# Moving ScalarE's share of the split forms within a unit, and an output's scaling across the seam between images (fp32 attention block, one core)

## The chip, the cores and the metric

The kernel runs on one core of a Trainium2 chip. The time is the device time of one execution in microseconds, the median of several runs. Engines are named as in the profile: PE (TensorE matmul), PEld (TensorE weight load), DVE (VectorE), ACT (ScalarE), POOL (GpSimd) and SP (SyncE). Each engine executes its own instructions in the order in which the program issues them, which for this kernel is written out by hand.

## The reference

The input is four images of 64 x 64 positions with 256 channels, in fp32. A layer computes self-attention in each image, and adds it to its input:

```python
q = jnp.einsum('bwhc,cd->bwhd', x, Wq) + bq      # 128 channels
k = jnp.einsum('bwhc,cd->bwhd', x, Wk) + bk      # 128 channels
v = jnp.einsum('bwhc,cd->bwhd', x, Wv) + bv      # 256 channels
pq = q.reshape(B, -1, N)                         # N = 4096
pk = k.reshape(B, -1, N)
pv = v.reshape(B, -1, N)
energy = jnp.einsum('bcn,bcm->bnm', pq, pk)
attention = jax.nn.softmax(energy, axis=-1)
out = jnp.einsum('bcm,bnm->bcn', pv, attention)
return gamma * out.reshape(B, W, H, C) + x
```

So for each image there is a 4096 x 4096 matrix of energies with 128 terms each, a softmax over its rows, and a product with v of 256 rows.

## The kernel before, in words

**Split operands.** Products of fp32 numbers are put together from three products of numbers in the faster fp32r format. Each operand of a product is split into three forms: a rounded one, what is left over, and a combination of both. The first form is an ACT instruction (a scaling that writes fp32r), the other two are DVE instructions that read the first. For q and k this is `halved` (ACT L263, DVE L265), for v it is `halve_v` (ACT L288 writes vh, DVE L291 writes vl and vd), and for the exponentials it is `upper` (ACT L343 writes h) and `halves` (DVE L349 writes l, L352 writes d).

**An image's work.** First its projection, 16 steps: PE transposes a part of x (tile xt, copied by ACT L130 into xts), multiplies it with the weights of q and k (tile qk, brought out by DVE L146 as qks) and of v (ACT L167). k's three forms and the plain q go to DRAM by DMA. After the projection come 128 units u, in 16 groups g of 256 rows of energies each, 8 units t to a group. A unit takes 512 columns.

**A unit.** In unit u the program issues, in this order: the energies of unit u + 3 (`LOOK`), in two halves k = 0 and 1; after the first half the `join` and `upper` of unit u + 2; then the steps of outputs in progress (`proceed`); `halves` of unit u + 1; in some units q's or v's forms; and `attend`, which multiplies unit u's h, l and d with vh, vl and vd. On each engine this comes to the following in a unit:

- PE: 12 matmuls for energies (tiles sa and sb, L324), then 24 for the output (tiles a with h and l, tile bb with d, L374).
- ACT: exponentials x and y of the first half (L328), h of unit u + 2 (L343), exponentials of the second half.
- DVE: the join of unit u + 2, x times y (L338), then l and d of unit u + 1 (L349, L352).

The tiles sa and sb have two buffers each in PSUM, so that PE may write the second half of the next unit's energies only when ACT has read the second half of this one's.

**The extra work in some units.** When the energies that a unit issues are the sixth unit of their group (`ahead % NU == 5`, which is u % 8 == 2) and there is a next group, the next group's q gets its forms: `halve_q`, 15 times an image (the first group's q is done in the projection). In units u = 1 and u = 3 of each image the last two parts of v get theirs: `halve_v`. In the kernel before both calls stand behind the whole energies of the unit, `proceed` and `halves`.

**Outputs.** A finished group's output goes through `finish`, a generator that takes one step at each `proceed`; a unit calls it twice. Its steps: ACT brings the sums out of PSUM (tile o, L385), DVE adds bb (L400), ACT scales by the reciprocal sums (L403), PE transposes (tile ot, L411), DVE adds the input (L415), and a DMA writes it. The last output of an image is in the middle of these steps when the next image's projection begins. Between the two images (called the seam below) stand these lines:

```python
            if b + 1 < B:
                proceed()
                images[b + 1].transposed(1)
                project_qk(b + 1, 0)
                proceed()
```

In the second `proceed` ACT issues the scaling of the last output (L403). `project_qk` issues q's and k's product and the forms of its k (ACT L263, which waits for qks).

Of the kernel before, what the change touches and what calls it, by code (L numbers as in the profile page):

```python
# [20 lines left out]
def kernel(  # L21
# [40 lines left out]
    C2 = C // 2  # L62
    NM = N // P
    KC = C // P
    NI = NM // 2
# [14 lines left out]
    def load_x(pool, b, g):  # L80
        t = pool.tile([P, 2, XB], F32, tag="x", name=f"x_{b}_{g}")
        nc.sync.dma_start(t, xv[b, g])
        return t
# [93 lines left out]
    NG = N // NB  # L177
    NU = NM // 4
# [22 lines left out]
    with ExitStack() as fast:  # L201
# [24 lines left out]
        images, qd, kf, units, loads, now = [], {}, {}, {}, {}, {}  # L226
# [5 lines left out]
        def start(pieces):  # L232
            active.append(pieces)
            next(pieces)

        def proceed():
            for pieces in list(active):
                if next(pieces, StopIteration) is StopIteration:
                    active.remove(pieces)
# [20 lines left out]
        def halved(f, x):  # L260

            h = f[:, :, 0, :]
            nc.scalar.activation(h, x, AF.Identity, scale=UPPER / 64)  # L263
            for j, s, op in ((1, -64.0, ALU.add), (2, 64.0 * (1.0 + E), ALU.subtract)):
                nc.vector.scalar_tensor_tensor(  # L265
                    f[:, :, j, :], h.bitcast(F32), s, x, ALU.mult, op
                )

        def project_qk(b, i):
            images[b].qk(i)  # L270
            x = now["qk"]
            for s in range(2):
                nc.gpsimd.dma_start(qd[b, i // 2 + NG // 2 * s][:, i % 2, :], x[:, s, :C2])  # L273
            f = kpool.tile([P, 2, 3, P], F32R, tag="f", name=f"f_{b}_{i}", bufs=2)
            halved(f, x[:, :, C2:])
            nc.gpsimd.dma_start(kf[b, i // 2][:, i % 2], f.rearrange("p s j d -> p s (j d)"))

        def project_v(b, i):
            images[b].v(i)
            units[b, "v4", i] = now["v4"]  # L280
            if i < NI - 2:
                halve_v(b, i)

        def halve_v(b, i):
            v4 = units.pop((b, "v4", i))
            m = slice(2 * i, 2 * i + 2)
            h = vh[:, m, :C]
            nc.scalar.activation(h, v4, AF.Identity, scale=UPPER * E)  # L288

            for t, f in ((vl, 1.0 / E), (vd, 1.0 / E + 1.0)):  # L290
                nc.vector.scalar_tensor_tensor(  # L291
                    t[:, m, :C], h.bitcast(F32), -f, v4, ALU.mult, ALU.add
                )

        def load_q(b, g):
            t = work.tile([P, NJ, P], F32, tag="qr", name=f"qr_{b}_{g}", bufs=1)
            nc.sync.dma_start(t, qd[b, g])
            loads[b, "qr", g] = t

        def halve_q(b, g):  # L300
            t = work.tile([P, 3, NJ, P], F32R, tag="q", name=f"q_{b}_{g}")
            halved(t.rearrange("p f j d -> p j f d"), loads.pop((b, "qr", g)))
            loads[b, "q", g] = t

        def load_k(b, u):
            if u < STEPS:
                t = kpool.tile([P, 4, 3, P], F32R, tag="k", name=f"k_{b}_{u}")
                nc.gpsimd.dma_start(t.rearrange("p (i s) f d -> p i s (f d)", s=2), kf[b, u % NU])  # L308
                loads[b, "k", u] = t

        def energy(b, u, k):

            g, t = divmod(u, NU)
            if k == 0:
                x = ppool.tile([P, 4, NB], F32, tag="x", name=f"x_{b}_{u}", bufs=3)
                y = ppool.tile([P, 4, NB], F32, tag="y", name=f"y_{b}_{u}")
                units[b, u] = x, y
            x, y = units[b, u]
            q, kt = loads[b, "q", g], loads[b, "k", u]
            sa = ps_s.tile([P, 2, NJ, P], F32, tag="a", name=f"sa_{b}_{u}_{k}")  # L320
            sb = ps_s.tile([P, 2, NJ, P], F32, tag="b", name=f"sb_{b}_{u}_{k}")
            for i in range(2):
                for to, f, first, last in ((sa, 0, True, False), (sa, 1, False, True), (sb, 2, True, True)):
                    nc.tensor.matmul(  # L324
                        to[:, i], kt[:, 2 * k + i, f, :], q[:, f], start=first, stop=last
                    )
            for to, sp, scale in ((x, sa, (1.0 + E) / E), (y, sb, -1.0 / E)):
                nc.scalar.activation(  # L328
                    to[:, 2 * k : 2 * k + 2, :],
                    sp.rearrange("p i j d -> p i (j d)"),  # L330
                    AF.Exp,
                    scale=scale,
                )

        def join(b, u):

            x, y = units[b, u]
            nc.vector.tensor_tensor(x, x, y, ALU.mult)  # L338
            units[b, u] = x

        def upper(b, u):
            h = ppool.tile([P, 4, NB], F32R, tag="h", name=f"h_{b}_{u}", bufs=3)
            nc.scalar.activation(h, units[b, u], AF.Identity, scale=UPPER)  # L343
            units[b, u] = units[b, u], h
# [117 lines left out]
        def begin(b, i):  # L462

            if i == 5:
                load_q(b, 0)
            if i == 9:
                halve_q(b, 0)
            if i in (4, 6, 8):
                load_k(b, i // 2 - 2)
            if i >= 10:  # L470
                energy(b, (i - 10) // 2, i % 2)
            if i in (12, 14):
                join(b, i // 2 - 6)
            if i in (13, 15):
                upper(b, i // 2 - 6)
                load_k(b, i // 2 - 3)

        image(0)
        for b in range(B):
            pr = images[b]  # L480
            if b == 0:
                now["banks"] = energies
                pr.transposed(0)
                pr.transposed(1)
                project_qk(b, 0)
            for i in range(1, NI):
                if i == 3:
                    now["banks"] = outputs
                if i + 1 < NI:
                    pr.transposed(i + 1)  # L490
                while i == 1 and active:
                    proceed()
                begin(b, i)
                project_qk(b, i)
                if i == NI - 1:
                    halves(b, 0)
                project_v(b, i - 1)
                proceed()
            project_v(b, NI - 1)
            for u in range(STEPS):  # L500
                g, t = divmod(u, NU)
                ahead = u + LOOK
                if ahead // NU + 1 < NG and ahead % NU == 3:
                    load_q(b, ahead // NU + 1)
                if u == STEPS - NU and b + 1 < B:
                    image(b + 1)
                if u >= STEPS - 3 and b + 1 < B:
                    now["banks"] = energies
                    if u == STEPS - 3:
                        images[b + 1].load(0)  # L510
                    elif u == STEPS - 2:
                        images[b + 1].transposed(0)
                if t == NU - 3:
                    loads[b, "x", g] = load_x(xpool, b, g)
                for k in range(2):
                    if ahead < STEPS:
                        energy(b, ahead, k)
                    if k == 0 and u + 2 < STEPS:
                        join(b, u + 2)
                        upper(b, u + 2)  # L520
                load_k(b, ahead + 2)
                proceed()
                if u + 1 < STEPS:
                    halves(b, u + 1)
                if ahead // NU + 1 < NG and ahead % NU == 5:
                    halve_q(b, ahead // NU + 1)

                if u in (1, 3):
                    halve_v(b, NI - 2 + u // 2)
                attend(b, u)  # L530
                if (b, u) == (B - 1, STEPS - 1):
                    finish_last(b, g, loads.pop((b, "x", g)))
                elif t == NU - 1:
                    start(finish(b, g, now["o"], now["bb"], loads.pop((b, "x", g))))
                proceed()
            if b + 1 < B:
                proceed()
                images[b + 1].transposed(1)
                project_qk(b + 1, 0)
                proceed()  # L540

    NB = 512
    NG = N // NB
# [3 lines left out]
    with tc.If(nc.values_load(again[0:1, 0:1]) > 0), ExitStack() as general:  # L547
# [8 lines left out]
        for b in range(B):  # L556
# [16 lines left out]
            for g in range(NG):  # L573
                ps = []
                mx = work.tile([P, 2, NB], F32, tag="mx", name=f"gmx_{b}_{g}")
                for t in range(NP):
# [9 lines left out]
                    p = ppool.tile([P, 2, NB], F32, tag="p", name=f"gp_{b}_{g}_{t}")  # L586
# [89 lines left out]
```

## Time and profile before

| | before |
|---|---|
| time, median of 3 runs | 2463.58 us (2461.89 to 2464.12) |
| span of the profiled execution | 2461.6 us |
| PE busy | 2444.7 us, 99% |
| PEld busy | 2410.5 us, 98% |
| DVE busy | 2096.1 us, 85% |
| ACT busy | 1802.1 us, 73% |
| POOL busy | 424.5 us, 17% |
| ACT, forms of q (L263, q) | 64 of 435 ns |
| ACT, forms of k (L263, f) | 64 of 417 ns |
| ACT, forms of v (L288, vh) | 64 of 630 ns |
| ACT, scalings of outputs (L403) | 126 of 527 ns |

Busy time is the time in which an engine had at least one instruction under way. An instruction's row gives the mean length of one. Instructions of one engine overlap a little, so that the step from one start to the next can be shorter than the length. Idle time in front of an instruction is put down to the engine and tile that released it last.

### The profile page before, as it was taken

The numbers are of one execution on the slowest core, as the hardware profiler recorded it, in microseconds if no ns is written. First come the engines' busy times: TensorE is split into PE (matmuls) and PEld (weight loads), VectorE is DVE, ScalarE is ACT, GpSimd is POOL, SyncE is SP. The second block draws the span as 40 slices with busy tenths as digits, with TensorE's granted clock in tenths as the row PEclk, the third lists the DMA queues.
The fourth block names the chain that finished last, engine by engine and source line by source line (L and its number), as shares of the span: only waits on it lengthen the run. The fifth ranks groups of instructions, "written<-read, shape, count | busy, mean of one in ns | idle before, by whom it ended". The sixth has DMA issues, their size and how long they took to land.

```text
span 2461.6 us, 50024 instructions
## 1 busy us (share of the span) xinstructions
PE 2444.7 (99%) x19982; PEld 2410.5 (98%) x19982; DVE 2096.1 (85%) x2314; ACT 1802.1 (73%) x3201; POOL 424.5 (17%) x781
## 2 busy tenths in 40 slices
PE   9999999999999999999999999999999999999998
PEld 8999999999899999999989999999998999999998
DVE  5888888888698888888869888888886988888887
ACT  5777777777677777777667777777766777777775
POOL 4211111111411111111141111111114111111110
PEclk9999999999999999999999999999999999999999
DMA  7666666665776666666477666666647766666663
GB/s 230 214 208 205 211 203 198 206 212 156 224 221 200 205 210 203 210 196 212 143 239 220 201 201 211 202 210 200 206 142 239 222 208 197 209 202 210 205 201 112
DMA packets 137408, 498.92 MB, mean 203 GB/s; under 512 B 15536, under 2 KB 57264, under 8 KB 137168
## 3 DMA queue, kind: packets, MB, share of 16 engines
q0 software_dynamic: 92320, 453.17, 59.1%
q1 hardware_dynamic: 44304, 42.22, 5.6%
q8 instruction: 160, 2.62, 0.4%
q14 instruction: 80, 0.66, 0.1%
q10 hardware_dynamic: 544, 0.26, 0.0%
HBM read 445.25 MB, written 50.33 MB: 201 GB/s over the span
## 4 chain that ended last, share of the span: by engine, by line


## 5 line engine op out<-in xcount | busy, mean ns | idle before, releaser
L328 ACT ACTIVATE x<-sa 128x512 f32<-128x512 f32 x1024 | 611.1, 597 | 498.1 <-PE sa L324 495.0
L338 DVE TENSOR_TENSOR x<-x,y 128x1024 f32<-128x1024 f32 x512 | 626.2, 1223 | 188.1 <-ACT y L328 188.1
L324 PE MATMUL sa<-q,k 128*128 128x256 f32 x4096 | 736.3, 279 | 1.1 <-ACT x L328 1.1
L352 DVE SCALAR_TENSOR_TENSOR d<-h,x 128x1024 fp32r<-128x1024 f32 x512 | 624.4, 1219 | 0.0
L349 DVE TENSOR_TENSOR l<-x,h 128x1024 fp32r<-128x1024 f32 x512 | 624.0, 1219 | 0.0
L324 PEld LDWEIGHTS sa<-q,k 128*128 128x128 f32 x4096 | 619.6, 188 | 2.2 <-ACT x L328 1.8
L328 ACT ACTIVATE y<-sb 128x512 f32<-128x512 f32 x1024 | 614.9, 600 | 0.0
L374 PE MATMUL a<-vh,h 128*128 128x258 f32 x4096 | 574.3, 283 | 0.0
L374 PE MATMUL a<-vl,l 128*128 128x258 f32 x4096 | 572.9, 282 | 0.0
L324 PE MATMUL sb<-q,k 128*128 128x256 f32 x2048 | 567.5, 277 | 0.0
L343 ACT ACTIVATE h<-x 128x1024 fp32r<-128x1024 f32 x512 | 544.1, 1063 | 22.6 <-DVE x L338 19.3
L374 PE MATMUL bb<-vd,d 128*128 128x256 f32 x4096 | 558.6, 279 | 0.0
L308 POOL DMA_DIRECT2D k<-kf x512 | 279.2, 545 | 1576.5 <-PE sb L324 1551.6
L374 PEld LDWEIGHTS a<-vl,l 128*128 128x128 f32 x4096 | 525.4, 189 | 0.0
L374 PEld LDWEIGHTS a<-vh,h 128*128 128x128 f32 x4096 | 522.9, 189 | 0.0
L374 PEld LDWEIGHTS bb<-vd,d 128*128 128x128 f32 x4096 | 515.1, 188 | 0.0
L324 PEld LDWEIGHTS sb<-q,k 128*128 128x128 f32 x2048 | 384.6, 188 | 0.9 <-ACT y L328 0.8
L137 PE MATMUL qk<-wqk_sb,xts 128*128 128x256 f32 x512 | 122.6, 383 | 0.0
L158 PE MATMUL v<-xts,wv_sb 128*128 128x256 f32 x512 | 120.3, 379 | 0.0
L158 PEld LDWEIGHTS v<-xts,wv_sb 128*128 128x128 f32 x512 | 97.3, 190 | 13.2
L137 PEld LDWEIGHTS qk<-wqk_sb,xts 128*128 128x128 f32 x512 | 93.4, 192 | 10.4
L273 POOL DMA_DIRECT2D qd<-qks x128 | 68.9, 544 | 184.9 <-DVE qks L146 175.7
(56 smaller groups left out, 868.6 us busy)
## 6 DMA issues: line engine op xcount, KB each, us to landing
k<-kf POOLq DMA_DIRECT2D x512, 768.0 KB, 4.7
x<-in_x_dram SPq DMA_DIRECT2D x128, 256.0 KB, 3.5
kf<-f POOLq DMA_DIRECT2D x64, 384.0 KB, 3.8
out_dram<-x POOLq DMA_DIRECT2D x63, 256.0 KB, 2.5
qd<-qks POOLq DMA_DIRECT2D x128, 64.0 KB, 2.9
qr<-qd SPq DMA_DIRECT2D x64, 128.0 KB, 2.6
wv_sb<-in_L_conv_Wv_dram POOLq DMA_DIRECT2D x1, 256.0 KB, 5.5
out_dram<-x SPq DMA_DIRECT2D x1, 256.0 KB, 4.1
```

The costliest lines, as they stand in the source:

```text
L137: nc.tensor.matmul(qk[:, s, :], self.xt[i][:, k, s, :], wqk_sb[:, k, :], start=(k == 0), stop=(k == KC - 1),)
L158: nc.tensor.matmul(vp[:, eh, :], wv_sb[:, k, eh * P : (eh + 1) * P], self.xt[i][:, k].rearrange("p s a -> p (s a)"), start=(k == 0), stop= ...
L273: nc.gpsimd.dma_start(qd[b, i // 2 + NG // 2 * s][:, i % 2, :], x[:, s, :C2])
L308: nc.gpsimd.dma_start(t.rearrange("p (i s) f d -> p i s (f d)", s=2), kf[b, u % NU])
L324: nc.tensor.matmul(to[:, i], kt[:, 2 * k + i, f, :], q[:, f], start=first, stop=last)
L328: nc.scalar.activation(to[:, 2 * k : 2 * k + 2, :], sp.rearrange("p i j d -> p i (j d)"), AF.Exp, scale=scale,)
L338: nc.vector.tensor_tensor(x, x, y, ALU.mult)
L343: nc.scalar.activation(h, units[b, u], AF.Identity, scale=UPPER)
L349: nc.vector.tensor_tensor(l, x, h.bitcast(F32), ALU.subtract)
L352: nc.vector.scalar_tensor_tensor(d, h.bitcast(F32), 1.0 + E, x, ALU.mult, ALU.subtract)
L374: nc.tensor.matmul(out_, left[:, i, j * P : (j + 1) * P], right[:, m, : out_.shape[1]], start=(t == i == 0 and (left is h or left is d and ...
```

## The change

The change moves instructions of ACT and leaves those of the other engines in their order. `halved` and `halve_v` become generators with two steps: the first issues the ACT instruction, the second the two DVE instructions. In a unit with such forms the first step is now taken between the first half of the energies and `join` and `upper`; the second stays where both stood. ACT's instruction so runs behind the exponentials of the first half and ahead of h, where it was behind the exponentials of the second half. The aim is that DVE finds the first form ready when it comes to the other two.

At the seam, the second `proceed` moves in front of `project_qk`, so that ACT issues the scaling of an image's last output in front of the form of the next image's first k, which has to wait for a product.

```diff
@@ halved @@
             nc.scalar.activation(h, x, AF.Identity, scale=UPPER / 64)
+            yield
             for j, s, op in ((1, -64.0, ALU.add), (2, 64.0 * (1.0 + E), ALU.subtract)):
                 nc.vector.scalar_tensor_tensor(
                     f[:, :, j, :], h.bitcast(F32), s, x, ALU.mult, op
                 )
+            yield
@@ halve_v @@
             nc.scalar.activation(h, v4, AF.Identity, scale=UPPER * E)
+            yield
 
             for t, f in ((vl, 1.0 / E), (vd, 1.0 / E + 1.0)):
                 nc.vector.scalar_tensor_tensor(
                     t[:, m, :C], h.bitcast(F32), -f, v4, ALU.mult, ALU.add
                 )
+            yield
@@ halve_q @@
-            halved(t.rearrange("p f j d -> p j f d"), loads.pop((b, "qr", g)))
             loads[b, "q", g] = t
+            yield from halved(t.rearrange("p f j d -> p j f d"), loads.pop((b, "qr", g)))
@@ the loop over units @@
+                beside = []
+                if ahead // NU + 1 < NG and ahead % NU == 5:
+                    beside.append(halve_q(b, ahead // NU + 1))
+                if u in (1, 3):
+                    beside.append(halve_v(b, NI - 2 + u // 2))
                 for k in range(2):
                     if ahead < STEPS:
                         energy(b, ahead, k)
+                    if k == 0:
+                        for forms in beside:
+                            next(forms)
                     if k == 0 and u + 2 < STEPS:
                         join(b, u + 2)
                         upper(b, u + 2)
...
                 proceed()
                 if u + 1 < STEPS:
                     halves(b, u + 1)
-                if ahead // NU + 1 < NG and ahead % NU == 5:
-                    halve_q(b, ahead // NU + 1)
-
-                if u in (1, 3):
-                    halve_v(b, NI - 2 + u // 2)
+                for forms in beside:
+                    next(forms)
                 attend(b, u)
@@ the seam @@
             if b + 1 < B:
                 proceed()
                 images[b + 1].transposed(1)
+                proceed()
                 project_qk(b + 1, 0)
-                proceed()
```

The other callers of these generators (in the projection) run them through at once, so that there the order is as before.

More of the change, by code (lines that the diff above doesn't have):

```diff
@@ L274, in project_qk @@
             f = kpool.tile([P, 2, 3, P], F32R, tag="f", name=f"f_{b}_{i}", bufs=2)
-            halved(f, x[:, :, C2:])
+            for _ in halved(f, x[:, :, C2:]):
+                pass
             nc.gpsimd.dma_start(kf[b, i // 2][:, i % 2], f.rearrange("p s j d -> p s (j d)"))
@@ L281, in project_v @@
             if i < NI - 2:
-                halve_v(b, i)
+                for _ in halve_v(b, i):
+                    pass
         def halve_v(b, i):
@@ L466, in begin @@
             if i == 9:
-                halve_q(b, 0)
+                for _ in halve_q(b, 0):
+                    pass
             if i in (4, 6, 8):
```

## The prediction

> **What bounds the kernel now.** I read the page's busy table first, then the list of waits, then two stretches of the timeline, then the busy table by stretches. The page and, below it, the list of waits (engine and line, who is waited for: total us, times, longest us):
>
> ```profile
> PE 2444.7 (99%) x19982; PEld 2410.5 (98%) x19982; DVE 2096.1 (85%) x2314; ACT 1802.1 (73%) x3201; POOL 424.5 (17%) x781
> ```
> ```profile
> DVE x L338 <- ACT y L328: 188.1, 304, 0.7
> ...
> DVE q L265 <- ACT q L263: 50.1, 60, 0.9
> DVE vl L291 <- ACT vh L288: 47.4, 64, 1.4
> ...
> ACT h L343 <- DVE x L338: 19.3, 16, 1.6
> ...
> PE ot L411 <- ACT o L403: 3.6, 3, 1.2
> ...
> PE sa L324 <- ACT x L328: 1.1, 4, 0.3
> ```
>
> PE sets the time almost everywhere: 2461.6 - 2444.7 = 16.9 us without a matmul in the whole span. So the change, which only reorders ACT, is worth no more than the PE holes that ACT causes. The long waits in this list (50.1 us of DVE on q's form) cost nothing by themselves; the two short PE rows are the ones to follow. They are two places. The first is the seam between images (timeline; start us, us, engine, line; idle before in brackets):
>
> ```profile
> 618.09 0.69 DVE L400 TENSOR_TENSOR o<-o,bb 128x512 f32<-128x512 f32 x1
> ...
> 618.52 0.59 ACT L130 COPY xts<-xt 128x512 f32<-128x512 f32 x1 [0.98 <-PE xt L124]
> 620.05 0.60 PE L124 MATMUL xt<-ident,x 128*128 128x128 f32 x4
> ...
> 620.98 0.42 ACT L263 ACTIVATE f<-qks 128x256 fp32r<-128x256 f32 x1 [1.87 <-DVE qks L146]
> ...
> 621.30 0.89 ACT L403 ACTIVATE o<-o,r 128x256 f32<-128x256 f32 x2
> 621.85 0.95 PE L411 MATMUL ot<-ident,o 128*128 128x128 f32 x4 [1.19 <-ACT o L403]
> ```
>
> The reader is to see that the scaling (L403) had its input at 618.09 + 0.69 = 618.78, and ACT was free at 618.52 + 0.59 = 619.11, but it stood behind k's first form (L263), which waited until 620.98 for qks. PE waited behind both. The second is unit u=5 of each image:
>
> ```profile
> 704.28 0.69 DVE L291 SCALAR_TENSOR_TENSOR vl<-vh,v 128x512 fp32r<-128x512 f32 x1 [0.41 <-ACT vh L288]
> ...
> 705.50 1.22 DVE L338 TENSOR_TENSOR x<-x,y 128x1024 f32<-128x1024 f32 x1
> ...
> 706.81 1.06 ACT L343 ACTIVATE h<-x 128x1024 fp32r<-128x1024 f32 x1 [1.58 <-DVE x L338]
> ...
> 707.77 0.58 ACT L328 ACTIVATE x<-sa 128x512 f32<-128x512 f32 x1
> ...
> 708.40 0.50 PE L324 MATMUL sa<-q,k 128*128 128x256 f32 x2 [0.27 <-ACT x L328]
> ```
> ```profile
> 703.04:707.29 4.25, 4.25 (x38) 4.25 (x37) 3.84 (x5) 2.67 (x6) 0.53 (x1) 1.00 0.82 246
> 707.29:712.33 5.04, 4.77 (x38) 4.39 (x37) 5.04 (x6) 4.66 (x8) 0.53 (x1) 1.00 0.53 166
> ```
>
> The last two rows are units u=4 and u=5 (stretch, length, then PE, PEld, DVE, ACT busy): u=5 takes 5.04 where its neighbours take 4.19 to 4.25. Reading backwards: PE may overwrite the PSUM tile sa only after ACT's exponential of 707.77 has read it; that exponential stood behind h, h behind the join L338, and the join behind DVE's parts of v's form, because DVE had waited 0.41 us for vh and earlier 0.19 for q and 0.34 for vh.
>
> **What the Trainium skill says.** "Perfetto Trace Analysis", Identifying the Most-Contended Engine: a busy PE is no measure of nearness to its peak, the share of LDWEIGHTS is a better one. Here both are at 98 to 99%, so PE is the bound on either. "TensorE: Matmul & The Clock Gate", Part 1 (architectural detail): ScalarE and VectorE take their queues strictly in order. The trace agrees: the scaling, ready at 618.78, ran at 621.30, after a form that waited. "ScalarE: Activation LUTs", What ACT_TABLE_LOAD costs: back-to-back ACTIVATEs overlap by about 93 ns; here x at 707.77 of 0.58 is followed by y at 708.25, an overlap of 0.10. I use the trace's durations.
>
> **The change part by part.** The order of PE, DVE, POOL and SP does not change, nor any operand. On ACT 71 items move: 60 forms of q (15 an image), 8 of v (u=1 and u=3), and 3 seams. Nothing is added or removed.
>
> *The seams.* With the scaling ahead of the form, it follows the copy: 619.11 to 619.11 + 0.89 = 620.00. PE comes to the ot transposes when the xt ones have gone in, about 620.05 + 4 x 0.11 = 620.5, by my reading of the matmul starts 0.11 us apart in such a group. So the wait ends with 0.5 us to spare. Start to start, PE went from the last xt to the first ot in 1.47 us, where two transposes of one group are 0.11 apart: 1.36 saved. The third ot waited for the second scaling: 0.40 instead of 0.11: 0.29 more. Sum 1.65 us a seam, x3 = 4.95 us. The form f now comes after, but its input arrives at 620.94, when the scaling is over, so it isn't delayed; and xts of 622.10 comes earlier. x tiles that the next transposes need had landed well before (PE shows no wait for a load there).
>
> *The stall at u=5.* I replay ACT and DVE of one first group with the trace's step from one start to the next (join, l and d 1.14; vl and vd 0.61; q's two parts 0.34; h 0.97; exponentials 0.48; vh 0.53; q 0.35), and PE units of 4.22 from 690.36. u=1: vh runs at 692.15 behind y, so DVE finds it ready after d and does vl at 694.38 instead of 694.81; the join of u=2 starts 695.60 (was 696.02). u=2: q runs at 696.34, h at 696.9, the pair of second exponentials ends at 698.9 (was 699.37); DVE's q parts start at 699.0 (was 699.71), the join of u=3 at 699.7 (was 700.38). u=3: vh at 700.56, h at 701.1, vl at 703.1 (was 704.28), the join of u=4 at 704.3 (was 705.50). u=4: h at 705.6 (was 706.81), second exponentials at 706.55 and 707.0, the first read done at 707.1. PE needs that buffer at 707.24 + 0.68 = 707.92, so there are 0.8 us in hand and the stall goes. The four u=5 units lost 5.04, 5.04, 4.99 and 5.02 against 4.20 in later groups: 3.3 us. Two u=6 units ran 0.06 slow in its wake: 0.1. Sum 3.4 us. The new waits: h is now queued behind vh or q, and behind h the second exponentials. At u=2 of a later group that puts them 0.35 later, to end about 1006.86, where PE needs the buffers from 1007.5: hidden by PE's own first six energy matmuls.
>
> *The 60 steady q's.* DVE no longer idles 0.88 us before q's parts (50.1 us in all). DVE has slack in the group: after u=4 it waits for the exponentials in each unit again (0.5 to 0.7 us), and PE never waits there. So nothing on the path. But unit lengths differ a little without any wait: u=3 takes 4.22, u=4 4.26, u=5 to u=7 4.19 to 4.21. In u=4 the twelve energy matmuls are 118 ns apart, in the others 113. What switches between the two rates I could not find (neither DVE, ACT nor DMA activity sorts them), so I bound it. Best: u=3 and u=4 fall to 4.193, saving 0.087 x 60 = 5.2 us. Worst: u=2, whose second exponentials now reach into u=3, becomes slow at its end and at the start of u=3, 0.075 x 60 = 4.5 us lost. I take 0.
>
> Sum: 4.95 + 3.4 = 8.35 us, 2463.58 - 8.35 = 2455.2.
>
> **Rivals.**
> 1. The matmul rates move too, for the better: 2455.2 - 5.2 = 2450.0. For it: DVE in u=3 runs as in the regular units again. Against: no cause is known.
> 2. They move for the worse: 2455.2 + 4.5 = 2459.7. For it: ACT's y now overlaps u=2's last matmuls. Against: u=5 of the third image has the same overlap and isn't slow.
> 3. Only one of the two holes closes. If DVE's 0.84 us excess over a unit still reaches u=5, only the seams gain: 2458.6. If the ot transposes meet another wait (a PSUM buffer, the copy), only u=5 gains: 2460.2. Against: 0.8 and 0.5 us in hand.
> 4. Slower: h and the second exponentials behind q and vh arrive too late and PE waits in each of the 60 + 8 units. If all of the moved time were exposed: 0.35 x 60 + 0.53 x 8 = 25 us, less 8.35: 2480. Against: each PSUM tile pair has 0.7 us in hand or more.
>
> **How the numbers follow.** Forecast 0.57, rival 1 0.20, rival 2 0.11, rival 3 0.09, rival 4 0.03. Faster by 0.2% means under 2458.65: the forecast, rival 1 and about half of rivals 2 and 3, where smaller shifts fall short of their full sizes: 0.85. Slower 0.03, the rest 0.12. The range runs from rival 1's end, 2450.0, to rival 2's, 2459.7.
>
> **What would show it.** Right: no PE wait on ACT's o (3.6 us now) and none of sa on x in the four u=5 units, unit u=5 at about 4.2 us, DVE's 50.1 us wait for q nearly gone while PE's steady units stay as they are. Wrong: a new PE wait on x or y at u=3, or steady groups of eight units that differ by more than 0.05 us from the present 34.13.

## The result, and the profile after

| | before | after |
|---|---|---|
| time, median of 6 runs each | 2463.51 us | 2453.45 us |
| lowest and highest | 2461.89 to 2464.12 | 2452.96 to 2455.39 |
| ratio, 95% interval | | 0.9963 (0.995 to 0.9976) |
| span of the profiled execution | 2461.6 us | 2451.3 us |

10.1 us less, where 8.35 were forecast. In the changed file the lines lie further down: the exponentials are L334, h is L349, the join L344, l and d L355 and L358, vh L292, vl and vd L296, the energies L330, the scaling of an output L409 and its transposes L417. The page's busy table of the changed kernel:

```profile
PE 2438.7 (99%) x19982; PEld 2408.0 (98%) x19982; DVE 2099.0 (86%) x2314; ACT 1795.2 (73%) x3201; POOL 424.5 (17%) x781
```

PE had 2461.6 - 2444.7 = 16.9 us without a matmul, and has 2451.3 - 2438.7 = 12.6. In the list of waits of the changed kernel (engine, line, who is waited for: total us, times, longest us) these are the rows that answer to those shown before:

```profile
DVE x L344 <- ACT y L334: 234.4, 416, 0.7
...
DVE vl L296 <- ACT vh L292: 44.5, 56, 1.4
...
ACT h L349 <- DVE x L344: 7.8, 8, 1.4
```

DVE's wait of 50.1 us for q is gone. It has not become time: the wait for the exponentials has grown from 188.1 to 234.4 us. DVE merely idles elsewhere. What counted are the two rows that are missing, PE's wait for the output o (3.6 us) and for the exponential x (1.1 us). They understate the gain, because PE's busy time for the same matmuls has fallen too, by 6.0 us. 2.4 of these lie in the first microseconds, which come last in this section. For the others, a stall can show as busy time: u=5 of the second image was 5.04 us long before, with 4.77 busy, and takes 4.2 now.

The first seam of the changed kernel, in its timeline (start us, us, engine, line):

```profile
615.33 0.69 DVE L406 TENSOR_TENSOR o<-o,bb 128x512 f32<-128x512 f32 x1
...
615.76 0.59 ACT L130 COPY xts<-xt 128x512 f32<-128x512 f32 x1 [0.98 <-PE xt L124]
...
616.24 0.91 ACT L409 ACTIVATE o<-o,r 128x256 f32<-128x256 f32 x2
617.29 0.60 PE L124 MATMUL xt<-ident,x 128*128 128x128 f32 x4
...
617.73 0.60 PE L417 MATMUL ot<-ident,o 128*128 128x128 f32 x4
...
618.22 0.42 ACT L263 ACTIVATE f<-qks 128x256 fp32r<-128x256 f32 x1 [1.06 <-DVE qks L146]
```

The scaling now follows the copy and ends at 617.15, before PE has even begun the xt transposes, which precede those of the output. The ot transposes follow the xt ones after 0.44 us, where it was 621.85 - 620.05 = 1.80. k's form (L263), now behind the scaling, starts right after its input is there, so it is not delayed.

Units u=4 and u=5 of the second image, from the same timeline, then their busy table (stretch, length, then PE, PEld, DVE, ACT and POOL busy, granted clock, DMA share and rate):

```profile
698.62 0.68 DVE L296 SCALAR_TENSOR_TENSOR vl<-vh,v 128x512 fp32r<-128x512 f32 x1
...
699.83 1.21 DVE L344 TENSOR_TENSOR x<-x,y 128x1024 f32<-128x1024 f32 x1
...
701.07 1.06 ACT L349 ACTIVATE h<-x 128x1024 fp32r<-128x1024 f32 x1 [0.61 <-DVE x L344]
...
702.04 0.58 ACT L334 ACTIVATE x<-sa 128x512 f32<-128x512 f32 x1
...
703.52 0.39 PE L330 MATMUL sa<-q,k 128*128 128x256 f32 x2
```
```profile
698.59:702.85 4.26, 4.26 (x39) 4.26 (x38) 4.26 (x6) 2.94 (x6) 0.53 (x1) 1.00 0.75 221
702.85:707.04 4.19, 4.19 (x38) 4.19 (x37) 4.19 (x5) 3.26 (x6) 0.53 (x1) 1.00 0.64 199
```

There is no bracket behind vl any more: DVE went on without a wait. ACT's exponential had read its PSUM tile at 702.04 + 0.58 = 702.62, and PE came for it at 703.52, with 0.9 us to spare. u=5 takes 4.2 us where it took 5.04.

Where the 10.3 us between the two profiles lie can be read from the first energy matmul of each image's unit u=1 in the timelines: 79.19, 690.36, 1301.77, 1912.85 before and 77.32, 685.91, 1294.72, 1903.36 after. The stretches between them shrank by 2.58, 2.61 and 2.43 us, the last image with its end by 0.8: 8.4 us in all, beside the 8.35 forecast. The remaining 1.87 us lie ahead of unit u=1 of the first image, where the change does nothing. The same product of the first step, before and then after:

```profile
7.66 3.52 PE L137 MATMUL qk<-wqk_sb,xts 128*128 128x256 f32 x8
```
```profile
7.42 1.89 PE L137 MATMUL qk<-wqk_sb,xts 128*128 128x256 f32 x8
```

Eight matmuls took 3.52 us in one execution and 1.89 in the other. The clock records of the traces, which tell what clock PE was granted, have the full clock from 10.95 us on in the first and from 5.62 us on in the second.

### The profile page after: what moved, and what is told of

Read it like the earlier page. It is cut to its first block, busy times and chain, and to the rows that moved or that the text cites. A ratio compares the mean times of both kernels' runs of the same rounds, so it can differ in the third digit from the quotient of the medians.

```text
span 2451.3 us, 50024 instructions
## 1 busy us (share of the span) xinstructions
PE 2438.7 (99%) x19982; PEld 2408.0 (98%) x19982; DVE 2099.0 (86%) x2314; ACT 1795.2 (73%) x3201; POOL 424.5 (17%) x781
## 4 chain that ended last, share of the span: by engine, by line
## 5 line engine op out<-in xcount | busy, mean ns | idle before, releaser
L334 ACT ACTIVATE x<-sa 128x512 f32<-128x512 f32 x1024 | 612.2, 598 | 516.1 <-PE sa L330 514.0
L344 DVE TENSOR_TENSOR x<-x,y 128x1024 f32<-128x1024 f32 x512 | 626.2, 1223 | 234.4 <-ACT y L334 234.4
L330 PE MATMUL sa<-q,k 128*128 128x256 f32 x4096 | 735.4, 279 | 0.0
L358 DVE SCALAR_TENSOR_TENSOR d<-h,x 128x1024 fp32r<-128x1024 f32 x512 | 623.3, 1217 | 0.0
L355 DVE TENSOR_TENSOR l<-x,h 128x1024 fp32r<-128x1024 f32 x512 | 623.2, 1217 | 0.0
L330 PEld LDWEIGHTS sa<-q,k 128*128 128x128 f32 x4096 | 619.4, 188 | 0.4
L334 ACT ACTIVATE y<-sb 128x512 f32<-128x512 f32 x1024 | 615.7, 601 | 0.0
L330 PE MATMUL sb<-q,k 128*128 128x256 f32 x2048 | 567.1, 277 | 0.0
L349 ACT ACTIVATE h<-x 128x1024 fp32r<-128x1024 f32 x512 | 543.8, 1062 | 8.3 <-DVE x L344 7.8
L330 PEld LDWEIGHTS sb<-q,k 128*128 128x128 f32 x2048 | 384.5, 188 | 0.1
```

Source lines behind the costliest of these rows:

```text
L330: nc.tensor.matmul(to[:, i], kt[:, 2 * k + i, f, :], q[:, f], start=first, stop=last)
L334: nc.scalar.activation(to[:, 2 * k : 2 * k + 2, :], sp.rearrange("p i j d -> p i (j d)"), AF.Exp, scale=scale,)
L355: nc.vector.tensor_tensor(l, x, h.bitcast(F32), ALU.subtract)
L358: nc.vector.scalar_tensor_tensor(d, h.bitcast(F32), 1.0 + E, x, ALU.mult, ALU.subtract)
```

## The experiments

**Each half of the change alone.** First the seam alone on the kernel before:

```diff
                 images[b + 1].transposed(1)
+                proceed()
                 project_qk(b + 1, 0)
-                proceed()
```

> The kernel before with the seam's second step moved in front of the next image's q and k product, the forms as before. My theory (two separate PE holes): about 1.65 us a seam, 4.95 us in all off the kernel before, ratio about 0.998; unit u=5 of each image still takes about 5.0 us; no wait of PE for o is left. Rival (the gain is that DVE is freed of its waits for q in every group): the seam gives next to nothing, and the steady groups of eight units bring the rest.

Measured: 2458.56 us beside 2463.78 of the kernel before, ratio 0.998 (0.997 to 0.9989), 5.2 us less. PE's wait for o is gone, and u=5 of the second image has its hole still:

```profile
704.64:709.56 4.92, 4.74 (x38) 4.35 (x37) 4.92 (x5) 4.56 (x8) 0.53 (x1) 1.00 0.52 167
```

Then the forms alone, which is the changed kernel with the seam's two lines put back:

> The changed kernel with the seam put back as before. My theory: 3.4 us off the kernel before, ratio about 0.9986, all of it in unit u=5 (5.0 to 4.2 us) and the unit after it; PE waits 1.2 us for o at each of three seams as before. Rival (freed DVE in every group): nearly the whole 8 to 10 us.

Measured: 2460.41 us beside 2463.78, ratio 0.9987 (0.998 to 0.9993), 3.4 us. u=5 is at 4.20 us in all four images, and at the three seams PE waits for o as before, 3.6 us in all.

5.2 + 3.4 = 8.6 us: the two halves add up, to what was forecast and not to the 10.1 measured. The rival, that freeing DVE in every group brings the gain, has fallen.

**Which forms matter.** v's two forms an image, or q's fifteen, each without the other and without the seam. The diff is against the kernel with the forms alone; the other variant keeps q's lines and puts v's back in the same way:

```diff
-                if ahead // NU + 1 < NG and ahead % NU == 5:
-                    beside.append(halve_q(b, ahead // NU + 1))
                 if u in (1, 3):
                     beside.append(halve_v(b, NI - 2 + u // 2))
...
                 for forms in beside:
                     next(forms)
+                if ahead // NU + 1 < NG and ahead % NU == 5:
+                    for _ in halve_q(b, ahead // NU + 1):
+                        pass
                 attend(b, u)
```

> Only v's forms (u=1 and u=3) are moved; q's and the seam are as before. My theory, by the same replay: DVE gains 0.43 us at u=1 and 0.4 to 0.5 at u=3, which is enough: u=5 at 4.2 us in all four images, as with all forms moved. Rival (q's 60 forms matter): u=5 improves in part and the steady units differ from the changed kernel.

> Only q's forms are moved; v's and the seam are as before. My theory: the 50 us of DVE's waits for q go, and yet just 0.28 us is gained an image: u=5 falls from 5.0 to about 4.75 us, all other units stay within 0.01 us. Rival (DVE's waits for q are on the path): 0.1 us or more in each of 60 units with a q form.

These two variants, and the three after them, were run once each, at 2461.8 to 2463.0 us. Single times tell little within a spread of 3.7 us (29 executions of the kernel before), so the unit lengths in the traces are read.

Measured with v's alone: u=5 at 4.20 us in all four images, though DVE still waits for q:

```profile
DVE q L266 <- ACT q L263: 49.5, 56, 0.9
```
```profile
707.20:711.40 4.20, 4.20 (x38) 4.20 (x37) 4.20 (x5) 3.37 (x6) 0.53 (x1) 1.00 0.60 178
```

With q's alone that wait is gone altogether, and u=5 is at 4.64 to 4.67 us, the same unit being

```profile
707.53:712.17 4.64, 4.64 (x38) 4.35 (x37) 4.64 (x5) 4.28 (x8) 0.53 (x1) 1.00 0.55 172
```

The steady groups have not moved by 0.01 us in either. So 49.5 us of DVE waiting left in place cost nothing, and 4 moved forms of q (the first of each image) have a part in the gain only if v's are not moved. The other 56 have none.

**One form of v at a time**, with `u == 1` or `u == 3` in the new place and the other in the old:

> Only the form of v at u=1 is moved (q's, the other of v and the seam as before). My theory, by the replay: 0.43 us of DVE's lateness gone, not quite enough; u=5 falls from about 5.0 to about 4.45 us (4.3 to 4.6). Rival (one part of v alone carries the whole stall): u=5 either 4.2 or unchanged at 5.0.

> Only the form of v at u=3 is moved. My theory: 0.49 us of lateness gone, u=5 at about 4.4 us (4.2 to 4.55). Rival as for u=1: 4.2 or 5.0.

Measured: u=5 at 4.51 to 4.53 with the first, and at 4.45 to 4.49 with the second. The same unit of the second image in these two kernels, one fence each:

```profile
707.61:712.12 4.51, 4.51 (x39) 4.33 (x37) 4.51 (x5) 4.17 (x8) 0.53 (x1) 1.00 0.58 166
```
```profile
706.12:710.61 4.49, 4.49 (x38) 4.31 (x37) 4.49 (x5) 4.11 (x8) 0.53 (x1) 1.00 0.58 186
```

Each of the three early forms so takes away a part of 0.3 to 0.6 us of one and the same lateness of about 0.84 us. Both of v's fill the hole, none does alone. The replay had 4.45 and 4.4, and 4.75 for q: right within 0.1 us.

**What the unit lengths depend on.** The prediction left open what makes u=3 and u=4 of a group a little longer than other units. Here the blocks of k and v are taken in another order from the second group on:

```diff
-                nc.gpsimd.dma_start(..., kf[b, u % NU])
+                nc.gpsimd.dma_start(..., kf[b, (u + 4 * (u >= NU)) % NU])
...
-                        m = 2 * t + i // 2 + NI * (i % 2)
+                        m = 2 * ((t + 4 * (g > 0)) % NU) + i // 2 + NI * (i % 2)
```

> The changed kernel, but from the second group of rows on the eight blocks of k and v are taken in the order 4 to 7, 0 to 3 (sums in another order, nothing left out). It asks what makes units u=3 and u=4 of each group 0.03 and 0.06 us longer without a wait. If it is the addresses of v that a unit reads, the slow ends of units u%8=1 and 3 move to u%8=5 and 7, and the slow energies to the units after those. If it is the place of the instructions in the program or what ACT and DVE do there, the unit lengths stay: 4.22, 4.64, 4.22, 4.25, 4.20, 4.19, 4.21, 4.19.

Measured: in the second half of a group (u % 8 = 5, 6, 7, 0) the pattern has moved by four units, while ACT's and DVE's extra work stayed where it was. That half in the changed kernel, then u % 8 = 2 and 3 and the second half with the blocks exchanged:

```profile
873.48:877.68 4.20, 4.20 (x39) 4.20 (x37) 3.46 (x4) 3.00 (x5) 0.53 (x1) 1.00 0.67 189
877.68:881.87 4.19, 4.19 (x38) 4.19 (x37) 3.48 (x4) 3.00 (x5) 0.53 (x1) 1.00 0.56 197
881.87:886.08 4.21, 4.21 (x39) 4.21 (x37) 3.51 (x4) 3.44 (x7) 0.53 (x1) 1.00 0.64 188
886.08:890.27 4.19, 4.19 (x38) 4.19 (x37) 4.12 (x8) 3.54 (x8) 0.00 (x0) 1.00 0.35 133
```
```profile
864.94:869.65 4.71, 4.71 (x43) 4.71 (x42) 4.50 (x7) 3.31 (x6) 1.25 (x2) 1.00 0.64 188
869.65:873.91 4.26, 4.26 (x39) 4.26 (x37) 3.79 (x4) 3.01 (x5) 0.54 (x1) 1.00 0.96 309
...
878.10:882.32 4.22, 4.22 (x39) 4.22 (x37) 3.53 (x4) 3.01 (x5) 0.53 (x1) 1.00 0.63 187
882.32:886.56 4.24, 4.24 (x38) 4.24 (x37) 3.49 (x4) 3.01 (x5) 0.53 (x1) 1.00 0.63 196
886.56:890.78 4.22, 4.22 (x39) 4.22 (x37) 3.50 (x4) 3.45 (x7) 0.53 (x1) 1.00 0.57 173
890.78:895.03 4.25, 4.25 (x38) 4.25 (x37) 4.18 (x8) 3.57 (x8) 0.00 (x0) 1.00 0.35 133
```

4.22, 4.24, 4.22 and 4.25 are the lengths that u=1 to u=4 had (u=2 in an image's first group, where it has no ot transposes). PE is busy in all of each, so no wait is in them. These lengths went along with the block of v that a unit reads. It is not what the block holds, since all four images show the same. k changes blocks too, but its three buffers turn with the unit, in no step of eight.

The block of v isn't the whole of it, however. u=2 and u=3 now read blocks that were read fast before, and yet take 4.71 and 4.26 us in this group, where the changed kernel has 4.63 and 4.22. In the groups that alternate with such ones they take 4.65 and 4.21, so that a group lasts 34.30 and 34.19 us in turn, beside 34.13. The blocks of v are the same in both kinds of group; what alternates from group to group are, among others, the two buffers of q and of the output. Which of them matters was not tried.

Two changes of the layout alone followed. In the first the rows of vh and vl get 258 instead of 260 elements (`VC = C + 2`), in the second the three unused tiles pad, pad2 and pad3 are left out:

> The changed kernel with rows of 258 instead of 260 elements in vh and vl, so that what stands behind them in the SBUF moves too; the same work. If addresses set the distance of matmuls (113 to 123 ns), the unit lengths of the steady groups change, in either direction, by some hundredths of a us up to 0.2 us a unit; if not, they stay at 4.22, 4.64, 4.22, 4.25, 4.20, 4.19, 4.21, 4.19.

> The changed kernel without its three small unused tiles between the pools, so that the tiles of exponentials, outputs and k lie 64, 512 and 704 bytes lower and v stays where it is; the same work. If it is the place of the operands of a matmul to each other that sets its distance, the unit lengths change; if it is v's addresses alone, they stay.

Measured, in one execution each and beside 2465.06 us for the kernel before: 2467.72 and 2497.49 us, where the changed kernel took 10 us less than the one before. The steady groups take 34.28 to 34.32 us with the shorter rows. The sum over a group in the changed kernel and without the pads:

```profile
sum 34.13, PE 34.13 PEld 34.13 DVE 30.14 ACT 25.69 POOL 4.42; mean PE 4.27 PEld 4.27 DVE 3.77 ACT 3.21 POOL 0.55
```
```profile
sum 34.80, PE 34.80 PEld 34.80 DVE 30.16 ACT 25.70 POOL 4.42; mean PE 4.35 PEld 4.35 DVE 3.77 ACT 3.21 POOL 0.55
```

DVE and ACT do the same work in the same time, and PE needs 0.67 us more for the same matmuls, 64 times: 43 us (from the first image's u=1 to the end the two traces differ by 41.5). v had not moved, only the tiles of exponentials, of q and the outputs, and of k. So it is not v's addresses alone, as the second expectation had as its alternative. Why one layout is slower than another is open.

**The first microseconds.** Six dummy matmuls more, on a tile that is ready sooner, in front of the twelve dummy transposes of the changed kernel, and in a second version three:

```diff
+        for _ in range(6):
+            nc.tensor.matmul(wp, ones, ones, start=True, stop=True)
         for _ in range(12):
             nc.tensor.transpose(wp, ident, ident)
```

> The changed kernel with six more dummy matmuls of the tile of ones in front of the twelve dummy transposes, from about 1.1 us on, when PE is idle anyway. My theory: the profiles of before and after differ by 1.9 us ahead of the first unit because the full clock was granted at 10.9 us in one and at 5.6 us in the other, by chance; with PE busy earlier the grant comes at about 5 us in nearly every execution, so the slower third of the times (2455.4) goes and the median stays near 2453.2. Rival (the difference ahead of the first unit comes from the change): the spread of times stays as it is.

> The changed kernel with three instead of six dummy matmuls ahead of the twelve transposes: they take about 0.73 us (2.93 for twelve halves in the run with six), so that the transposes of x start at about 5.3 us as in the changed kernel, not at 6.6. My theory: the full clock comes at 5 to 6.5 us in every execution and the time is about 2453.2 in all of them, 1.2 below the run with six and equal to the faster executions of the changed kernel; against the changed kernel's median about 0 to 0.5 us. Rival: with fewer dummies PE's activity isn't enough in some executions, and some of the times are near 2455.4 again.

Measured with six: 2454.43 us beside 2464.53, ratio 0.9959 (0.9945 to 0.9972), the five times within 2454.19 to 2454.51. The times are close together, but so were those of the kernel before that ran beside them (2463.96 to 2465.02), so this doesn't show an effect of the dummies. Nor is the gain on the kernel before larger than the changed kernel's: both are 10.1 us. In the trace, the first transposes start at 6.60 us instead of 5.31, but the second ones then wait 0.54 us for x and start at 7.80 instead of 6.92, so that here the load of x set the start. The full clock came at 6.41 us, not at about 5. With three: 2456.05 beside 2465.06, ratio 0.9962 (0.9948 to 0.9976), from 2454.36 to 2456.24. The three dummies took 1.65 us and not 0.73, the first transposes came at 4.87 us, and yet, in the timeline of that run:

```profile
4.87 0.66 PE L124 MATMUL xt<-ident,x 128*128 128x128 f32 x4
8.21 1.12 PE L124 MATMUL xt<-ident,x 128*128 128x128 f32 x4 [2.68 <-DMA x<-in_x_dram]
9.12 2.85 PE L137 MATMUL qk<-wqk_sb,xts 128*128 128x256 f32 x8
```

The clock records have the full clock from 4.22 us, then half from 7.64 to 11.05. PE had it and lost it again while it waited 2.68 us for x. The expectation fell: the times are neither all alike nor at its 2453.2, and its rival, with some near 2455.4, described them better. None of these versions is shown to be faster than the changed kernel.

## Why the prediction was right, point by point

**The seams.** 1.65 us each were forecast, by two differences of starts. In the timelines, from the last energies of an image (u=124) to u=1 of the next, the three seams with their projection shrank by 1.69, 1.71 and 1.64 us: 5.04 against 4.95. The copy, the scaling and the transposes stand in the forecast order. The seam alone took off 5.2 us (4.9 from the first image's u=1 to the end of its trace).

**The stall at u=5.** 3.3 us were forecast for the four units and 0.1 in their wake. The units went from 5.04, 5.04, 4.99 and 5.02 to 4.20 each, together 3.3, and the forms alone took off 3.4 (3.2 in the trace, counted likewise). The replay can be checked in its steps: with the unit u=4 at 698.59 instead of 703.04, 4.45 us earlier, its join at 704.3, h at 705.6 and exponential at 706.55 should appear at 699.85, 701.15 and 702.1; they stand at 699.83, 701.07 and 702.04.

**The 60 steady forms.** Forecast as worth nothing, and the trials of q's and v's forms show it. The bounds that the prediction put around it, 5.2 us to the better and 4.5 to the worse, were for unit lengths that the change did not touch: the group of 34.13 us is the same to the hundredth.

**The rivals.** The time of 2453.45 us lies between the forecast and rival 1, and can't tell them apart. The steady groups can: 1 and 2 fell because these take 34.13 us before and after. The exchanged blocks and the layouts give a likely reason, that such lengths follow the operands' places, which this change leaves alone. 3 fell, both holes closed. 4 fell: no wait of PE on an exponential is left in the list.

**What the sum missed.** The 10.1 us measured are 1.7 more than forecast. The two profiles differ by 8.4 us from the first image's u=1 on, which is the forecast, and by 1.87 us ahead of it, with the same instructions and another moment of the full clock. The change has no part in that: nine traces, of the kernels before and after and of the seven variants up to the exchanged blocks, have the same instructions up to this point, and reach it at 77.32 to 80.34 us. The latest is that of the forms alone, and the profile of the changed kernel happens to have the earliest. That the medians, too, lie 1.7 us further apart for this reason is inferred from the profiles, not shown run by run.

## What to carry to other kernels

Start from the gaps of the engine that sets the time, however short they are in the list of waits, and follow each back to the instruction that something ready is queued behind. Here 4.7 us of such waits led to 8.6 us of gain, and 50 us of waits on another engine to none. An instruction that must wait for a long product belongs behind the short ones that are ready on its in-order engine. Lateness that builds up over several units is best replayed with the trace's steps, to see how much of it has to be taken away before the wait at its end is gone.

## What the runs showed of the hardware

Matmuls of the same form, at the full clock and without a wait, do not always follow each other at the same distance, and the layout of their operands has a part in it. In the group of the changed kernel shown above, the energies of most units stand 113.3 ns apart and those of u=4 117.8. Leaving out 704 bytes of unused tiles brought the energies of all units to 118 ns or more, and cost 0.67 us in each group of 34.13 us, some 43 us in all. A slow end of a unit went along with slow energies in the next: the last eight output products of u=3 stood 118.5 ns apart in that group, while those of u=4 to u=7, with fast energies behind them, stood 114.5 to 116.2 apart. (Behind u=1, with 118.0, the ot transposes come first.)

The full PE clock at the start is not kept by having been given once. In three of the thirteen traces it was withdrawn 3.41 us after it came, and PE had been busy for 1.25 us (three dummies), 1.40 us (the form at u=1 alone) and 1.55 us (q's forms alone) of that stretch. In the ten others it stayed, and the least busy of these, with the form at u=3 alone, had PE busy for 1.67 us of it.
